# A 4-layer graph network on one core: the first transposes of 26 of 32 states go from TensorE to VectorE and DRAM, and the written-out order is chosen from sixteen

## The chip, the cores and the metric

The kernel runs on one core of a Trainium2 chip, in float32. The metric is the device time of one execution in microseconds (us), as a median of three runs. Five engines work side by side, each through its own list of instructions, in order: TensorE (PE in the profile, its weight loads PEld), VectorE (DVE), ScalarE (ACT), GpSimd (POOL) and SyncE (SP), which here issues nearly all DMAs. Within an engine nothing overtakes; between engines semaphores make an instruction wait for what it reads.

## The reference

32 states `x[b]` of 512 tokens x 128 features pass four residual layers that share one 512 x 512 adjacency. Each layer begins with a layer norm and a relu. Cut to what matters here:

```python
# layer 0
h = relu(layernorm(x));  x = x + (A_norm @ h) @ W.T + b
# layer 1: five recurrent steps, in_matrix and out_matrix are both adj
h = relu(layernorm(x))
for _ in range(5):
    m  = adj @ h;  av = concat([m, m])
    u3 = h @ u3_w.T + u3_b
    z  = sigmoid(av @ w3_w.T + w3_b + u3)
    r  = sigmoid(av @ w4_w.T + w4_b + u3)
    hv = tanh(av @ w5_w.T + w5_b + (r * h) @ u5_w.T + u5_b)
    h  = (1 - z) * h + z * hv
x = x + h
# layers 2 and 3: attention over the edges of adj (softmax), then x = x + elu(out) or x + out
```

## The kernel before

**Forms of a state.** A state is kept with tokens on partitions (`x`, `h`) or with features on partitions (`hT`). The products with the adjacency read `h` and give `m`, which has features on partitions; the gates of a recurrent step read `m` and `hT`. So each state needs both forms at the beginning of layer 1, and each of the first four steps has to turn its new `hT` back into an `h`.

**Layer 0 (`gcn`, L526).** States go in pairs. The first pair (states 0 and 1) uses `product` (L516): for each state four matmuls 128x512 against `anT`, then one ScalarE copy. All other pairs use `products` (L461): two states together in seven block products instead of eight, by sums and differences. That takes 14 matmuls 128x256 for the pair, four VectorE combinations (`combine`, L473), three VectorE sums (`add_up`, L498) and four ScalarE copies (`copy`, L490), and needs four factors made beforehand from `anT` or `adjT` (`right_factors`, L309). A float32 matmul appears as two records in the profile; a transpose is one.

**Layer 1 (`ggnn`, L547, and `step`, L565).** At the start, `norm_relu` (L400, ScalarE at L407) writes `h`. Then `to_features` (L426) turns it with four TensorE transposes 128x128 (L432) into a PSUM bank, and ScalarE copies the bank into `hT` (L555). Each of five steps does `products` for the pair with the `adjT` factors, and per state the gate matmuls L569, L570 (which reads `hT`), L576, L583, L584, three ScalarE tanhs (L572, L578, L586) and four VectorE operations (L574, L588, L589, L591). `shuttle` (L436) turns the new `hT` back without TensorE: VectorE transposes 32x32 squares into `sq` (L442), four DMAs write `sq` to the DRAM buffer `far` (L449), and two or one more DMAs read it into `h` (L453, L457). There are two `sq` buffers and four `far` buffers. At most six states are in layer 1 at a time (`LANES`), that is three pairs.

**Layers 2 and 3 (`gat`, L621)** use the same shuttle for the input (`gT`, L446, L457), and matmuls L644 and L699. The last four states (`NEAR`) use TensorE transposes there (L629, L664, L688), as does a last stretch of layer 1 if it is due late.

**What sets the order.** All instructions are first collected as operations with an engine, a cost, a delay until the result is seen, and a due time. `Plan.run` (L81) then plays the whole kernel through as a list scheduler: for each engine, the ready operation with the earliest due time goes next, if its buffers are free. A due time is lowered to `last - tail * hurry` where that is earlier; `tail` is the length of the chain that follows, and `last` and `hurry` are 174 and 0.08 (L201). The order that comes out is the order in which every engine's instructions are written; the costs are the planner's own, the chip only gets the order. Each DMA is planned with a delay of 4 us (into `far`) or 5 us (out of it). Recurrent VectorE work has a due time 5 ahead of its step, ScalarE's has the step's own.

Of the kernel before, what the change touches and what calls it, by code (L numbers as in the profile page):

```python
# [2 lines left out]

# [15 lines left out]
W = 32  # L19
Q = P // W  # L20
NEAR = 4
EASE = 0
LANES = 6


# [17 lines left out]
class Plan:  # L43
# [2 lines left out]

    DELAY = {"PE": 0.24, "ACT": 0.15, "DVE": 0.12, "POOL": 0.1, "SP": 2.4, "AQ": 2.4}

    def __init__(self, buffers, last, hurry):
        self.buffers, self.last, self.hurry, self.ops = buffers, last, hurry, []  # L50

    def op(self, engine, cost, due, emit, r=(), w=(), delay=None):
        o = Op(engine, cost, due, emit, self.DELAY[engine] if delay is None else delay)
# [25 lines left out]
        self.ops.append(o)  # L79

    def run(self):  # L81
        free = {k: list(reversed(v)) for k, v in self.buffers.items()}
        ready = {e: [] for e in self.DELAY}
        busy = dict.fromkeys(self.DELAY, False)
        events, order, done = [], [], 0

        for o in reversed(self.ops):
            o.tail = o.cost + o.delay + max((q.tail for q in o.then), default=0)
            o.due = min(o.due, self.last - o.tail * self.hurry)
        for o in self.ops:  # L90
            if not o.waits:
                heapq.heappush(ready[o.engine], (o.due, o.id))
        now, count = 0.0, 0

        def post(t, kind, x):
            nonlocal count
            count += 1
            heapq.heappush(events, (t, count, kind, x))

        def start(e):  # L100
            if busy[e]:
                return
            kept = []
            while ready[e]:
                key = heapq.heappop(ready[e])
                o = self.ops[key[1]]
                opens = [v for v in o.vals if v.kind and v.t is None]
                short = [v for v in opens if len(free[v.kind]) < sum(u.kind == v.kind for u in opens)]
                if not short:
                    for v in opens:  # L110
                        v.t = free[v.kind].pop()
                    busy[e] = True
                    o.at = now
                    order.append(o)
                    post(now + o.cost, 0, o)
                    post(now + o.cost + o.delay, 1, o)
                    break
                kept.append(key)
            for key in kept:
                heapq.heappush(ready[e], key)  # L120

        def settle(o, same):
            for q in o.then:
                if (q.engine == o.engine == "PE") == same:
                    q.waits -= 1
                    if not q.waits:
                        heapq.heappush(ready[q.engine], (q.due, q.id))

        for e in ready:
            start(e)  # L130
        while events:
            now, _, kind, o = heapq.heappop(events)
            if kind == 0:
                busy[o.engine] = False
                settle(o, True)
            else:
                done += 1
                settle(o, False)
                for v in o.vals:
                    v.uses -= 1  # L140
                    if not v.uses and v.kind:
                        free[v.kind].append(v.t)
            for e in ready:
                start(e)
        assert done == len(self.ops), "the order has come to a stop"
        self.order, self.end = order, now
        for o in order:
            o.emit()


@with_exitstack
def gnn_stack(ctx: ExitStack, tc: tile.TileContext, a: dict, out: bass.AP):
# [13 lines left out]
    def flat(t):  # L166
# [31 lines left out]
        "rstd": tiles(8, SMALL, "rstd"),  # L198
        "off": tiles(4, SMALL, "off"),
        "rden": tiles(3, SMALL, "rden"),  # L200
    }, 174, 0.08)  # L201
    op = plan.op
    MM, MM1, TURN = 0.858, 0.224, 0.111
    V, A = 0.61, 0.585
# [94 lines left out]
    def right_factors(mT, due):  # L299
# [10 lines left out]
                f[k][0](), quarter(*u), quarter(0, 1) if v is None else f[v][0]()),  # L310
               r=[mT, *([f[v][1]] if v else [])], w=[f[k][1]])
        return f
    of_adj, of_an = right_factors(adjT, -3), right_factors(anT, -1)


    maskT = {l: fixed([P, Q, N], f"maskT{l}", C, dtype=BF16) for l in (2, 3)}
# [119 lines left out]
    def shuttle(src, squares, dst, halves, due, soon):  # L436
# [19 lines left out]
        else:  # L456
            op("SP", 0.4, due, lambda: nc.sync.dma_start(  # L457
                dst.t if dst.kind != "h" else dst.t.rearrange("p a (k f) -> p (a k) f", k=2), far.t.rearrange("q i k f -> (q i) k f")),
               r=[far], w=[dst], delay=5)

    def products(h1, h2, factors, due):  # L461

        x1, x2, S = (h1[0], h1[1]), (h2[0], h2[1]), Val("S", 4)
        HV, HM, HA = 0.34, 2 * 0.432, 0.26

        def part(item):
            v, a = item
            return v.t[:, a, :]  # L470

        def combine(o, u, v, f):
            op("DVE", HV, due - 5, lambda: f(part(o), part(u), part(v)), r=[u, v], w=[o])  # L473
        add, sub = nc.vector.tensor_add, nc.vector.tensor_sub
        combine(S[2], x1[0], x2[0], sub)
        combine(S[0], x2[0], x2[1], add)
        combine(S[1], S[0], x1[0], sub)
        combine(S[3], x1[1], S[1], sub)
        m1, m2, p1, u2, u4, r, t = Val("m", 2), Val("m", 2), Val("half"), Val("half"), Val("half"), Val("bank"), Val("bank")

        def times(r, item, k, fresh, *also):
            def two():
                u = part(item).rearrange("p (f l) -> p l f", l=2)
                for l in range(2):
                    nc.tensor.matmul(low(r), u[:, l, :], factors[k][0]()[:, l, :], start=fresh and l == 0, stop=l == 1,  # L485
                                     skip_group_check=not fresh)
            op("PE", HM, due, two, r=[item, factors[k][1]], w=[r, *also])

        def copy(o, r, out):
            op("ACT", HA, due, lambda: nc.scalar.copy(out(), low(r)), r=[r], w=[o])  # L490

        def low(v):
            return flat(v.t)[:, :2 * P]

        def high(v):
            return flat(v.t)[:, 2 * P:]
        def add_up(o, u, out):
            op("DVE", HV, due - 5, lambda: nc.vector.tensor_add(out(), u.t, low(t)), r=[u, t], w=[o])  # L498

        times(r, x1[0], 0, True, m1, m2, t, p1, u2, u4)  # L500
        copy(p1, r, lambda: p1.t)
        times(t, x1[1], 3, True)
        add_up(m1[0], p1, lambda: low(m1))
        times(r, S[1], 1, False)
        copy(u2, r, lambda: u2.t)
        times(t, S[2], 4, True)
        times(r, S[0], 2, False)
        copy(u4, r, lambda: u4.t)
        add_up(m2[1], u4, lambda: high(m2))
        times(t, x2[1], 6, False)  # L510
        add_up(m2[0], u2, lambda: low(m2))
        times(r, S[3], 5, False)
        copy(m1[1], r, lambda: high(m1))
        return m1, m2
# [9 lines left out]


    def gcn(pair, due):  # L526
        first, ys = pair[0] == 0, []
        for i, b in enumerate(pair):
            y = Val("y", C) if first else Val("pair", 2)
            norm_relu(b, y, 2 * b - 798 if first else due + i)  # L530
            op("DVE", V, due + i + 1, lambda b=b: nc.vector.tensor_add(
                xs[b].t, xs[b].t, b0.t[:, None, :].to_broadcast([P, C, D])), r=[b0], w=[xs[b]])
            ys.append(y)

        ms = [product(y, anT, due + i + 1) for i, y in enumerate(ys)] if first else products(*ys, of_an, due + 1)
        for i, (b, m) in enumerate(zip(pair, ms)):
            p = Val("bank")

            def out_mm(m=m, p=p):
                for c in range(C):  # L540
                    nc.tensor.matmul(p.t[:, c, :], m.t[:, c, :], w0T.t[:, 0, :], start=True, stop=True)  # L541
            op("PE", C * MM1, due + i + 1.5, out_mm, r=[m, w0T], w=[p])
            op("DVE", V, due + i + 1.5, lambda b=b, p=p: nc.vector.tensor_add(flat(xs[b].t), flat(xs[b].t), flat(p.t)),
               r=[p], w=[xs[b]])


    def ggnn(pair, due):  # L547
        hs, hTs, lanes = [], [], []
        for b in pair:
            lane, h, hT = Val("lane"), Val("h", 2), Val("hT")  # L550
            op("SP", 0.0, due - 3, lambda: None, r=[xs[b]], w=[lane], delay=0)
            op("SP", 0.0, due - 3, lambda: None, r=[lane], w=[h], delay=0)
            norm_relu(b, h, due - 3)
            p = to_features(h, due - 2, hT)
            op("ACT", A, due - 2, lambda p=p, hT=hT: nc.scalar.copy(flat(hT.t), flat(p.t)), r=[p], w=[hT])  # L555
            hs.append(h)
            hTs.append(hT)
            lanes.append(lane)
# [6 lines left out]
    def step(b, s, m, hT, due, lane):  # L565
        gate, r, rh, z = Val("bank"), Val("r"), Val("rh"), Val("z")

        def reset():
            nc.tensor.matmul(flat(gate.t), gates.t[:, 0, :], flat(m.t), start=True, stop=False)  # L569
            nc.tensor.matmul(flat(gate.t), gates.t[:, 1, :], flat(hT.t), start=False, stop=True)  # L570
        op("PE", 2 * MM, due + 0.2, reset, r=[m, hT, gates], w=[gate])
        op("ACT", A, due, lambda: nc.scalar.activation(flat(r.t), flat(gate.t), AF.Tanh, bias=gate_b["w4"].t, scale=0.5),  # L572
           r=[gate, gate_b["w4"]], w=[r])
        op("DVE", V, due - 5, lambda: nc.vector.scalar_tensor_tensor(flat(rh.t), flat(r.t), 1.0, flat(hT.t), op0=ALU.add, op1=ALU.mult),  # L574
           r=[r, hT], w=[rh])
        op("PE", MM, due + 0.3, lambda: nc.tensor.matmul(flat(gate.t), gates.t[:, 2, :], flat(m.t), start=False, stop=True,  # L576
                                                   skip_group_check=True), r=[m, gates], w=[gate])
        op("ACT", A, due, lambda: nc.scalar.activation(flat(z.t), flat(gate.t), AF.Tanh, bias=gate_b["w3"].t, scale=0.5),  # L578
           r=[gate, gate_b["w3"]], w=[z])
        cand, hv, new = Val("bank"), Val("hv"), Val("hT")  # L580

        def candidate():
            nc.tensor.matmul(flat(cand.t), gates.t[:, 3, :], flat(m.t), start=True, stop=False)  # L583
            nc.tensor.matmul(flat(cand.t), u5T.t[:, 0, :], flat(rh.t), start=False, stop=True)  # L584
        op("PE", 2 * MM, due + 0.4, candidate, r=[m, rh, gates, u5T], w=[cand])
        op("ACT", A, due, lambda: nc.scalar.activation(flat(hv.t), flat(cand.t), AF.Tanh, bias=gate_b["w5"].t),  # L586
           r=[cand, z, gate_b["w5"]], w=[hv])
        op("DVE", V, due - 5, lambda: nc.vector.tensor_sub(flat(hv.t), flat(hv.t), flat(hT.t)), r=[hT], w=[hv])  # L588
        op("DVE", V, due - 5, lambda: nc.vector.scalar_tensor_tensor(flat(hv.t), flat(z.t), 1.0, flat(hv.t), op0=ALU.add, op1=ALU.mult),  # L589
# [172 lines left out]
```

## Time and profile before

| | us |
|---|---|
| median of 3 runs | 1664.14 (1663.68 to 1665.16) |
| profiled execution, its own time | 1663.59 |
| its span, first to last instruction | 1661.8 |
| PE busy | 1634.7 |
| DVE busy | 1362.7 |
| ACT busy | 734.8 |
| POOL busy | 143.2 |

A busy time counts every moment in which at least one instruction of the engine is running. Matmuls overlap in the PE, so a row's mean duration (such as 593 ns) is longer than the distance from one matmul to the next. That distance has to be read from the starts in the timeline. "Idle before" in a row is the time that the engine had nothing running before the row's instructions, and the arrow names what ended it.

### The profile page before, as it was taken

To read this page: it belongs to the slowest core of one execution; us is meant where nothing else is said; L and a number is where in the kernel's file an instruction comes from. 1 tells how busy PE (TensorE), PEld (TensorE's weight loads), DVE (VectorE), ACT (ScalarE), POOL (GpSimd) and SP (SyncE) were. 2 spreads that over 40 slices of the span, in tenths; PEclk is the share of its full clock that TensorE was granted. 3 is DMA by queue.
4 is the path that set the end of the run, shared out by engine and by line. 5 is a ranking of instruction groups with operands and counts; after the bars stand their busy time and mean duration, and the time that the engine had idled before them with its cause. 6 is when DMAs were issued, how large, how long until landed. Compare 5 with 4: busy or idle time off the path is not lost.

```text
span 1661.8 us, 23750 instructions
## 1 busy us (share of the span) xinstructions
PE 1634.7 (98%) x7422; PEld 1176.3 (71%) x7422; DVE 1362.7 (82%) x3836; ACT 734.8 (44%) x1657; POOL 143.2 (9%) x136
## 2 busy tenths in 40 slices
PE   7999999999999999999999999999999999999998
PEld 5766667677776777777677776777777777766677
DVE  8966778888878888888788888888888878777888
ACT  4643453535345354433534335353443534333433
POOL 2200000001001110000100000000000000000100
PEclk9999999999999999999999999999999999999999
DMA  5222333433334343342423334333242423434100
GB/s 153 51 70 58 83 83 95 115 80 99 90 89 108 84 105 87 91 113 73 122 71 99 98 92 108 90 96 95 77 121 64 108 70 91 106 90 114 27 26 27
DMA packets 311423, 146.17 MB, mean 88 GB/s; under 512 B 150400, under 2 KB 292864, under 8 KB 311296
## 3 DMA queue, kind: packets, MB, share of 16 engines
q1 hardware_dynamic: 311008, 144.12, 34.4%
q8 instruction: 59, 0.97, 0.2%
q14 instruction: 68, 0.56, 0.1%
q10 hardware_dynamic: 288, 0.52, 0.1%
HBM read 80.48 MB, written 64.08 MB: 87 GB/s over the span
## 4 chain that ended last, share of the span: by engine, by line
PE 92%; DVE 5%; ACT 1%; issue 1%; DMA 0%; POOL 0%; SPq 0%; DVEq 0%; POOLq 0%; ACTq 0%
PE bank L485 33%; PE bank L699 12%; PE bank L570 8%; PE bank L569 8%; PE bank L576 8%; PE bank L583 8%; PE bank L584 8%; PE bank L644 3%; PE bank L541 2%; PE bank L688 1%; PE bank L432 1%; DVE st L390 1%; PE bank L520 0%; ACT y L407 0%; POOL rstd L397 0%
## 5 line engine op out<-in xcount | busy, mean ns | idle before, releaser
L485 PE MATMUL bank<-made,S 128*128 128x256 f32 x1140 | 276.3, 380 | 3.9 <-DVE S L473 1.8
L397 POOL TENSOR_TENSOR rstd<-ve,mhalf 128x4 f32<-128x4 f32 x128 | 141.4, 1107 | 1491.0 <-DVE ve L395 1193.6
L485 PEld LDWEIGHTS bank<-made,S 128*128 128x128 f32 x1140 | 218.1, 196 | 45.5 <-issue 19.0
L490 ACT COPY half<-bank 128x256 f32<-128x256 f32 x285 | 105.3, 370 | 256.9 <-PE bank L485 254.9
L699 PEld LDWEIGHTS bank<-h_gat,e 128*128 128x128 f32 x1792 | 208.1, 192 | 12.7 <-issue 10.8
L572 ACT ACTIVATE r<-bank,gate_bw 128x512 f32<-128x512 f32 x160 | 109.6, 686 | 230.0 <-PE bank L570 218.7
L699 PE MATMUL bank<-h_gat,e 128*128 128x129 f32 x1792 | 208.5, 275 | 0.0
L574 DVE SCALAR_TENSOR_TENSOR rh<-r,hT 128x512 f32<-128x512 f32 x160 | 109.8, 687 | 100.6 <-ACT r L572 99.9
L679 DVE SCALAR_TENSOR_TENSOR e<-row,h_gat,maskT 128x512 f32<-128x512 f32 x256 | 181.3, 742 | 2.8 <-ACT row L666 2.8
L588 DVE TENSOR_TENSOR hv<-hv,hT 128x512 f32<-128x512 f32 x160 | 109.4, 683 | 67.6 <-ACT hv L586 67.2
L576 PE MATMUL bank<-m,wT 128*128 128x512 f32 x320 | 163.7, 593 | 0.0
L583 PE MATMUL bank<-m,wT 128*128 128x512 f32 x320 | 163.6, 593 | 0.0
L569 PE MATMUL bank<-m,wT 128*128 128x512 f32 x320 | 163.4, 592 | 0.0
L570 PE MATMUL bank<-hT,wT 128*128 128x512 f32 x320 | 163.4, 592 | 0.0
L584 PE MATMUL bank<-rh,wT 128*128 128x512 f32 x320 | 163.4, 592 | 0.0
L586 ACT ACTIVATE hv<-bank,gate_bw 128x512 f32<-128x512 f32 x160 | 109.5, 684 | 118.7 <-PE bank L584 117.5
L485 PE MATMUL bank<-adjT,h 128*128 128x256 f32 x640 | 157.8, 380 | 1.5 <-ACT h L407 1.5
L498 DVE TENSOR_TENSOR m<-half,bank 128x256 f32<-128x256 f32 x285 | 117.6, 413 | 43.2 <-ACT half L490 22.8
L485 PEld LDWEIGHTS bank<-adjT,h 128*128 128x128 f32 x640 | 121.7, 196 | 25.9 <-issue 12.1
L578 ACT ACTIVATE z<-bank,gate_bw 128x512 f32<-128x512 f32 x160 | 109.5, 684 | 49.5 <-PE bank L576 48.2
L390 DVE BATCH_NORM_STATS2 st<-x 128x6 f32<-128x128 f32 x512 | 121.6, 278 | 0.4
L570 PEld LDWEIGHTS bank<-hT,wT 128*128 128x128 f32 x320 | 60.8, 190 | 76.5 <-issue 76.5
(116 smaller groups left out, 2247.6 us busy)
## 6 DMA issues: line engine op xcount, KB each, us to landing
far<-sq SPq DMA_DIRECT2D x832, 64.0 KB
h<-far SPq DMA_DIRECT2D x248, 128.0 KB
gT<-far SPq DMA_DIRECT2D x56, 256.0 KB
row<-line SPq DMA_DIRECT2D x56, 256.0 KB
x<-in_x_dram SPq DMA_DIRECT2D x32, 256.0 KB
out_dram<-x SPq DMA_DIRECT2D x32, 256.0 KB
h<-far SPq DMA_DIRECT2D x28, 256.0 KB
far_mask<-mask SPq DMA_DIRECT2D x8, 128.0 KB
```

Of the source, the lines that this page charges most:

```text
L390: op("DVE", 0.21, due, lambda c=c: nc.vector.bn_stats(st.t[:, c, :], xb.t[:, c, :]), r=[xb[c]], w=[st[c]])
L397: op("POOL", 1.0, due, lambda: nc.gpsimd.tensor_tensor(rstd.t, ve.t, mhalf.t, ALU.pow), r=[ve, mhalf], w=[rstd])
L485: nc.tensor.matmul(low(r), u[:, l, :], factors[k][0]()[:, l, :], start=fresh and l == 0, stop=l == 1, skip_group_check=not fresh)
L498: op("DVE", HV, due - 5, lambda: nc.vector.tensor_add(out(), u.t, low(t)), r=[u, t], w=[o])
L569: nc.tensor.matmul(flat(gate.t), gates.t[:, 0, :], flat(m.t), start=True, stop=False)
L570: nc.tensor.matmul(flat(gate.t), gates.t[:, 1, :], flat(hT.t), start=False, stop=True)
L574: op("DVE", V, due - 5, lambda: nc.vector.scalar_tensor_tensor(flat(rh.t), flat(r.t), 1.0, flat(hT.t), op0=ALU.add, op1=ALU.mult), r=[r, h ...
L576: op("PE", MM, due + 0.3, lambda: nc.tensor.matmul(flat(gate.t), gates.t[:, 2, :], flat(m.t), start=False, stop=True, skip_group_check=Tru ...
L583: nc.tensor.matmul(flat(cand.t), gates.t[:, 3, :], flat(m.t), start=True, stop=False)
L584: nc.tensor.matmul(flat(cand.t), u5T.t[:, 0, :], flat(rh.t), start=False, stop=True)
L679: op("DVE", 0.68, due + 3, lambda j=j: nc.vector.scalar_tensor_tensor(e.t[:, j, :], row.t, h.t[:, j, D + 1:D + 2], maskT[l].t[:, j, :], op ...
L699: nc.tensor.matmul(pt()[:, c, :D + 1], e.t[:, j, i * P:(i + 1) * P], h.t[:, j, :D + 1], start=(j == 0), stop=(j == C - 1))
```

## The change

1. **First state by squares and DRAM.** For the states 2 to 27 (`FAR0 <= b < B - FAR1`) the transposes and the copy into `hT` are replaced by the new `shuttle_first`: two VectorE transposes of 32x32 squares from `h` to `sq`, four DMAs from `sq` to `far`, four DMAs from `far` to `hT`. States 0, 1 and 28 to 31 stay as they were. `hT` now has four parts, one for each DMA.
2. **Second pair in full.** States 2 and 3 use `product` with full matmuls in layer 0, like 0 and 1, and take their normed input from the two `y` buffers. The factors made from `anT` are due at 5 instead of -1.
3. **ScalarE ahead.** The recurrent tanhs are due 5 earlier, the copies in `products` 6 earlier.
4. **Order.** The planner tries sixteen pairs of `last` and `hurry` (170, 173, 176, 179 by 0.06, 0.08, 0.1, 0.12) and writes out the order that ends first by its own costs.

```diff
+FAR0, FAR1 = 2, 4
...
+        uses = {v: v.uses for o in self.ops for v in o.vals}
+        best = min(self.ends, key=lambda end: self.attempt(uses, *end))
+        self.attempt(uses, *best)
...
+    def attempt(self, uses, last, hurry):
...
+            o.soon = min(o.due, last - o.tail * hurry)
...
-    }, 174, 0.08)
+    }, [(last, hurry) for last in (170, 173, 176, 179) for hurry in (0.06, 0.08, 0.1, 0.12)])
...
-    of_adj, of_an = right_factors(adjT, -3), right_factors(anT, -1)
+    of_adj, of_an = right_factors(adjT, -3), right_factors(anT, 5)
...
+    def shuttle_first(h, hT, due, soon):
+
+        sq, far = Val("sq"), Val("far", Q)
+        for a in range(2):
+            op("DVE", 0.34, soon, lambda a=a: nc.vector.transpose(
+                sq.t.rearrange("p k (a l i) -> p a k l i", a=2, l=2)[:, a],
+                h.t.rearrange("p a (k j l) -> p a k l j", k=Q, l=2)[:, a]), r=[h[a]], w=[sq])
+        for q in range(Q):
+            op("SP", 0.44, due, lambda q=q: nc.sync.dma_start(
+                far.t[:, :, q, :].rearrange("k j f -> j k f"), sq.t[q * W:(q + 1) * W]), r=[sq], w=[far[q]], delay=4)
+        for q in range(Q):
+            op("SP", 0.4, due, lambda q=q: nc.sync.dma_start(
+                hT.t.rearrange("p c (q i) -> q p c i", q=Q)[q], far.t.rearrange("k j q (c i) -> q (k j) c i", c=C)[q]),
+               r=[far[q]], w=[hT[q]], delay=5)
...
-            op("ACT", HA, due, lambda: nc.scalar.copy(out(), low(r)), r=[r], w=[o])
+            op("ACT", HA, due - 6, lambda: nc.scalar.copy(out(), low(r)), r=[r], w=[o])
...
-        first, ys = pair[0] == 0, []
+        first, ys = pair[0] < 4, []
...
-            norm_relu(b, y, 2 * b - 798 if first else due + i)
+            norm_relu(b, y, 2 * b - 798 if pair[0] == 0 else due + i)
...
-            lane, h, hT = Val("lane"), Val("h", 2), Val("hT")
+            lane, h, hT = Val("lane"), Val("h", 2), Val("hT", Q)
...
-            p = to_features(h, due - 2, hT)
-            op("ACT", A, due - 2, lambda p=p, hT=hT: nc.scalar.copy(flat(hT.t), flat(p.t)), r=[p], w=[hT])
+            if FAR0 <= b < B - FAR1:
+                shuttle_first(h, hT, due - 2.5, due - 3)
+            else:
+                p = to_features(h, due - 2, hT)
+                op("ACT", A, due - 2, lambda p=p, hT=hT: nc.scalar.copy(flat(hT.t), flat(p.t)), r=[p], w=[hT])
...
-        op("ACT", A, due, lambda: nc.scalar.activation(flat(r.t), flat(gate.t), AF.Tanh, bias=gate_b["w4"].t, scale=0.5),
+        op("ACT", A, due - 5, lambda: nc.scalar.activation(flat(r.t), flat(gate.t), AF.Tanh, bias=gate_b["w4"].t, scale=0.5),
...
```

The tanhs of `z` and `hv` get the same `due - 5`.

More of the change, by code (lines that the diff above doesn't have):

```diff
@@ L1 @@
 import heapq
+import math
 from contextlib import ExitStack
@@ L47, with __init__ @@
     DELAY = {"PE": 0.24, "ACT": 0.15, "DVE": 0.12, "POOL": 0.1, "SP": 2.4, "AQ": 2.4}
-    def __init__(self, buffers, last, hurry):
-        self.buffers, self.last, self.hurry, self.ops = buffers, last, hurry, []
+    def __init__(self, buffers, ends):
+        self.buffers, self.ends, self.ops = buffers, ends, []
     def op(self, engine, cost, due, emit, r=(), w=(), delay=None):
@@ L81, in run @@
     def run(self):
+        for o in reversed(self.ops):
+            o.tail = o.cost + o.delay + max((q.tail for q in o.then), default=0)
+            o.first = o.waits
+        uses = {v: v.uses for o in self.ops for v in o.vals}
+        best = min(self.ends, key=lambda end: self.attempt(uses, *end))
+        self.attempt(uses, *best)
+        assert self.end < math.inf, "the order has come to a stop"
+        for o in self.order:
+            o.emit()
+    def attempt(self, uses, last, hurry):
+        for v, n in uses.items():
+            v.uses = n
+            if v.kind:
+                v.t = None
+        for o in self.ops:
+            o.waits = o.first
+            o.soon = min(o.due, last - o.tail * hurry)
         free = {k: list(reversed(v)) for k, v in self.buffers.items()}
@@ L85, in run @@
         events, order, done = [], [], 0
-        for o in reversed(self.ops):
-            o.tail = o.cost + o.delay + max((q.tail for q in o.then), default=0)
-            o.due = min(o.due, self.last - o.tail * self.hurry)
         for o in self.ops:
             if not o.waits:
-                heapq.heappush(ready[o.engine], (o.due, o.id))
+                heapq.heappush(ready[o.engine], (o.soon, o.id))
         now, count = 0.0, 0
@@ L126, in settle @@
                     if not q.waits:
-                        heapq.heappush(ready[q.engine], (q.due, q.id))
+                        heapq.heappush(ready[q.engine], (q.soon, q.id))
         for e in ready:
@@ L144, in run @@
                 start(e)
[L145 to L148, printed above, removed]
+        self.order, self.end = order, now if done == len(self.ops) else math.inf
+        return self.end
 @with_exitstack
@@ L577, in step @@
                                                    skip_group_check=True), r=[m, gates], w=[gate])
-        op("ACT", A, due, lambda: nc.scalar.activation(flat(z.t), flat(gate.t), AF.Tanh, bias=gate_b["w3"].t, scale=0.5),
+        op("ACT", A, due - 5, lambda: nc.scalar.activation(flat(z.t), flat(gate.t), AF.Tanh, bias=gate_b["w3"].t, scale=0.5),
            r=[gate, gate_b["w3"]], w=[z])
@@ L585, in step @@
         op("PE", 2 * MM, due + 0.4, candidate, r=[m, rh, gates, u5T], w=[cand])
-        op("ACT", A, due, lambda: nc.scalar.activation(flat(hv.t), flat(cand.t), AF.Tanh, bias=gate_b["w5"].t),
+        op("ACT", A, due - 5, lambda: nc.scalar.activation(flat(hv.t), flat(cand.t), AF.Tanh, bias=gate_b["w5"].t),
            r=[cand, z, gate_b["w5"]], w=[hv])
```

## The prediction

> **What bounds the kernel now.** I read the page's busy times first, then the busy times by stage.
>
> ```profile
> PE 1634.7 (98%) x7422; PEld 1176.3 (71%) x7422; DVE 1362.7 (82%) x3836; ACT 734.8 (44%) x1657; POOL 143.2 (9%) x136
> ...
> PE 92%; DVE 5%; ACT 1%; issue 1%; DMA 0%; POOL 0%; SPq 0%; DVEq 0%; POOLq 0%; ACTq 0%
> ```
>
> ```profile
> 0.00:20.00 20.00, 13.36 (x65) 9.96 (x66) 13.36 (x48) 8.95 (x20) 3.79 (x10) 1.00 0.74 209
> 20.00:40.00 20.00, 16.51 (x69) 11.64 (x68) 19.49 (x89) 10.08 (x25) 5.21 (x5) 1.00 0.30 90
> 40.00:60.00 20.00, 20.00 (x88) 14.98 (x87) 19.74 (x77) 14.35 (x34) 5.00 (x6) 1.00 0.40 103
> 60.00:80.00 20.00, 20.00 (x91) 16.11 (x90) 19.33 (x95) 13.18 (x33) 8.20 (x8) 1.00 0.09 21
> 300.00:1300.00 1000.00, 999.40 (x4562) 722.76 (x4561) 843.14 (x2370) 442.52 (x1001) 86.07 (x79) 1.00 0.38 95
> ```
>
> The columns are PE, PEld, DVE, ACT, POOL, clock, DMA share. From 300 to 1300 us the PE is idle for 0.6 us in 1000. It loses time at the ends: 10.1 us before 37 us, some 3.9 us between 1500 and 1570, and 10.8 us after 1612 (of which 4.9 lie behind the last matmul). Busy does not mean full speed, so I looked at the starts in the timeline of PE:
>
> ```profile
> 503.72 1.03 PE L485 MATMUL bank<-made,S 128*128 128x256 f32 x4
> 504.58 1.11 PE L432 MATMUL bank<-ident,h 128*128 128x128 f32 x8
> 505.53 1.90 PE L485 MATMUL bank<-adjT,h 128*128 128x256 f32 x8
> 507.27 1.04 PE L485 MATMUL bank<-adjT,S 128*128 128x256 f32 x4
> ```
>
> [...] The starts speak otherwise: four records start 0.86 us before the next row, eight 1.74 us, that is 0.215 to 0.2175 apart, without a hole. PE is full, by order and not only by record. I take the starts: a microsecond of work taken from PE between 40 and 1500 us is a microsecond off the end, as long as the others deliver.
>
> **The change part by part.**
>
> *First state, PE.* The eight transposes above are two states and occupy 505.53 - 504.58 = 0.95 us of PE. 26 of 32 states lose theirs: 13 x 0.95 = 12.35 us off PE. Four transposes alone take 0.43 us elsewhere (1544.57 to 1545.00), which would give 11.2; I take the row in the steady part. ScalarE loses 26 copies (L555, 586 ns), 15.2 us, worth nothing by itself: ScalarE is 44% busy and its waits are mostly for PE.
>
> *First state, DVE.* 52 square transposes are added. The nearest row is the same operation on a state of the same size:
>
> ```profile
> L432 PE MATMUL bank<-ident,h 128*128 128x128 f32 x128 | 19.8, 283 | 0.6 <-ACT h L407 0.6
> L555 ACT COPY hT<-bank 128x512 f32<-128x512 f32 x32 | 18.1, 586 | 1.9 <-PE bank L432 1.3
> L442 DVE STREAM_TRANSPOSE sq<-hT 128x256 f32<-128x256 f32 x248 | 105.5, 433 | 1.4
> ```
>
> 52 x 0.433 = 22.5 us. DVE in the middle is 84.3% busy; with 19 states there (76 of the 104 transposes) it gets 16.5 us more in about 990, 86.7%. Between 40 and 80 us DVE was 98% busy and PE still 100%, so this is covered. Without that cover, each state would hold PE for its two transposes, 0.87 us, 22.5 us in all. A gain is excluded for an added operation. Ends 0 and 22.5; the 40 to 80 us rows are the nearest, I take +0.5.
>
> *First state, SP and DMA.* 208 DMAs are added: 104 into `far` (L449, median 434 ns of SP) and 104 out of it with 512 pieces each (as L453, 524 ns): 45 + 54 = 99 us of issue. SP's two great groups now take 832 x 0.434 + 248 x 0.524 = 491 us of 1662, so the queue has room. It is in order, though: behind an L449 that waits stand the next `h` of other lanes (L453), the rows (L676), outputs (L721) and loads of `x` (L239). Such waits exist already:
>
> ```profile
> SPq L449 <- DVE sq L442: 189.6, 70, 16.4
> ...
> SPq L449 <- DMA h<-far: 83.9, 42, 2.8
> ```
>
> (total, times, longest). Waits up to 16.4 us there reach PE nowhere in the middle, where PE waits 0.6 us in all and not for a DMA. Two `sq` and four `far` buffers serve 124 + 84 = 208 shuttles; they get 26 more, an eighth. I put SP at 0.
>
> ```profile
> DMA packets 311423, 146.17 MB, mean 88 GB/s; under 512 B 150400, under 2 KB 292864, under 8 KB 311296
> ...
> q1 hardware_dynamic: 311008, 144.12, 34.4%
> ```
>
> 34.4% of 16 engines x 1661.8 us over 311,008 packets is 29.4 ns each. The last step writes `hT` in runs of 32 floats, 128 B: 2048 packets for a state, with 512 more into `far`. 26 x 2560 x 29.4 ns / 16 = 122 us, so the share rises by 7 points to 42%. One DMA of 512 packets needs 0.94 us. [...] The rows show 208 such turns in 1662 us, with runs of 256 B and more, at 34%. The squares are turned on DVE; the DMA moves whole runs. I take the trace.
>
> *The new wait.* L570 of a pair's first step will wait for DMAs instead of ScalarE. From `h`: 0.87 us on DVE; from the first L449 to the issue of L453 3.2 us (50.39 to 53.62); four issues 2.1; landing 2.8 by the longest wait above: 9.0 us. PE has the pair's seven products in between, 28 records x 0.2175 = 6.1 us; the other 2.9 us must come from the two other pairs in the lanes. The planner allows 4 and 5 us for the DMAs, more than these rows show, so its order leaves that room. Uncovered it would cost 13 x 2.9 = 38 us; I take 0. Queued behind a waiting L570 is all of PE.
>
> *Second pair.* Seven products, 28 x 0.2175 = 6.09 us, become eight matmuls 128x512, 16 records: four last from 18.90 to 20.61, 0.4275 each, 6.84. PE +0.75. DVE loses four combinations and three sums (7 x 0.41 = 2.9), and the four `anT` factors (683 ns each) move behind the first states, 2.7 us out of a stretch where DVE was 97% busy (20 to 40 us) and PE idle for 3.5. PE's waits from 24 us to 37 are 1.45, 0.22, 0.38, 0.19 and 0.50 us, 2.7 in all: the most to be gained. Two more states in the two `y` buffers and two shuttles may cost as much. I take -1.0.
>
> *ScalarE ahead, and the order.* No instruction is added. 860 ScalarE instructions get earlier due times than 480 norm-relus (L407) and the attention's L646, L673, L714; no DMA and no POOL work moves with them. PE's waits for ScalarE sum to some 8 us over the whole span, so this gains at most that; cover is ScalarE's 56% idle time, and without it norms come late. The choice among sixteen can reach PE's 5.9 us of waiting after 1612 and 3.9 at 1500 to 1570, about -9, and may miss by as much, since it goes by planned costs (V = 0.61 where the rows have 0.68). I take -0.5 for both together, near zero because no row shows it.
>
> *Sum.* -12.35 + 0.75 + 0.5 - 1.0 - 0.5 = -12.6 us. The profiled execution took 1663.59 us (span 1661.8 and 1.8 around it), so 1651.0; the median is 0.55 above that execution, so about 1651.5.
>
> **The rivals.**
>
> *DVE becomes the bound in places* (0.09). For: 98% at 20 to 80 us, its real operations longer than planned. Against: PE fed without a gap there. Half of the far end, 11 us, would come back: 1651.5 - 0.5 + 11 = 1662, or a third (7.5 us): about 1658.5. I put it at 1658 to 1662.
>
> *The order gives much more* (0.11). ScalarE ahead shortens the last states' recurrence, and the startup runs denser; of 5.9 + 3.9 + 2.7 us some 8 go instead of 1.5: 1645.
>
> *Slower: the first `hT` comes late* (0.03). One mechanism, at L570 of thirteen pairs: 2.9 us uncovered gives 1651.5 + 38 = 1689; slower from 12.6 / 13 = 0.97 us for a pair on. For: two `far` waits of 2.8 us exist, and small packets. Against: the planner's allowance.
>
> *The change does not do what it says* (0.02): the order chosen for its planned end is worse by 12 us on the chip than the one before: 1664. It would have to lose more than all waits at the end.
>
> **How the numbers follow.** The forecast has 0.75, with its own range 1647 to 1656. The range that should hold 8 in 10 takes in most of the better order and part of the DVE case: 1645 to 1659.5. A difference of 0.2%, 3.3 us, is about what a measurement of this kernel can tell from no change. Faster: 0.75 + 0.11 + two thirds of 0.09 = 0.92. Same: a third of 0.09 and the last rival, with some of the slower one's small end: 0.05. Slower: 0.03.
>
> **What would show it.** Right: L432 with h at 24 records instead of 128, L555 at 6, PE busy near 1621, PE again 99.9% in the middle, DVE near 86%, DMA share near 42%. Wrong: a wait of PE or PEld at L570 for a DMA `hT<-far` above a few us in total, SP waiting for `far` for hundreds of us with PE idle, or PE idle in the middle by over 5 us with DVE named. A time under 1645 would mean that the ends, not the transposes, brought most.

## The result, and the profile after

The changed kernel takes 1647.05 us (median of 5 runs, 1646.67 to 1649.17), the kernel before 1664.12 us beside it. The ratio is 0.9901, with a 95% interval of 0.9887 to 0.9915. The forecast was 1651.5 (1645.0 to 1659.5): right in direction and inside the range, but the gain is 17.1 us where 12.6 were added up. The profiled execution has a span of 1645.1 us, 16.7 less than before.

The page of the changed kernel: busy times, the chain that ended last, and the DMA queue that carries the shuttles.

```profile
PE 1620.7 (99%) x7306; PEld 1159.8 (71%) x7306; DVE 1373.5 (83%) x3881; ACT 722.0 (44%) x1629; POOL 144.6 (9%) x136
...
DMA packets 381312, 159.81 MB, mean 97 GB/s; under 512 B 206976, under 2 KB 362752, under 8 KB 381184
...
q1 hardware_dynamic: 380896, 157.77, 39.4%
...
PE 94%; DVE 4%; DMA 1%; issue 0%; ACT 0%; SPq 0%; DVEq 0%
```

PE's busy time fell by 14.0 us, to the 1621 of the forecast. DVE's rose by 10.8. The DMA share rose by 5.0 points, not 7: 69,888 packets more (2688 a state, where the forecast had 2560), but 0.394 x 16 x 1645.1 / 380,896 = 27.2 ns each instead of 29.4.

The groups of instructions of the changed kernel that stand for the first states (line, operation, count, busy, mean, idle before):

```profile
L448 PE MATMUL bank<-ident,h 128*128 128x128 f32 x24 | 3.5, 281 | 0.0
L589 ACT COPY hT<-bank 128x512 f32<-128x512 f32 x6 | 3.4, 580 | 0.2
L481 DVE STREAM_TRANSPOSE sq<-h 128x256 f32<-128x256 f32 x52 | 21.9, 432 | 0.1
```

24 transposes of `h` are left of 128, 6 copies of 32, and the 52 new squares last 432 ns each, as their neighbours did. The stages of the changed kernel (PE, PEld, DVE, ACT, POOL, clock, DMA share, GB/s; the clock is the granted share of TensorE's full clock):

```profile
0.00:20.00 20.00, 13.58 (x64) 10.57 (x65) 12.46 (x47) 8.75 (x20) 3.79 (x10) 1.00 0.76 211
20.00:40.00 20.00, 18.97 (x78) 12.50 (x77) 19.52 (x87) 10.17 (x26) 4.61 (x5) 1.00 0.30 85
40.00:60.00 20.00, 18.89 (x68) 11.79 (x67) 18.79 (x77) 12.59 (x30) 5.61 (x6) 1.00 0.56 135
60.00:80.00 20.00, 19.79 (x85) 14.85 (x84) 19.72 (x85) 11.95 (x31) 4.95 (x6) 1.00 0.43 87
300.00:1300.00 1000.00, 1000.00 (x4509) 719.53 (x4508) 863.36 (x2450) 447.95 (x1017) 92.19 (x82) 1.00 0.44 107
```

PE is busy for 18.97 us of the second 20 instead of 16.51. It gives 1.3 us of that back from 40 to 80, where it was full before. Between 300 and 1300 its records leave no gap. DVE is at 86.3% there, as forecast. SP's waits (total, times, longest):

```profile
SPq L465 <- DVE sq L458: 191.1, 63, 14.2
...
SPq L465 <- DMA h<-far: 67.6, 29, 3.7
...
SPq L485 <- DVE sq L481: 14.0, 7, 3.7
```

The old shuttles wait about as long as before for squares (191 us, 190 before) and less for a free `far` (68, 84 before). The new ones (L485) wait 14 us for squares and have no such row for `far`.

**A sharper measure than busy time.** A 128x256 record lasts 380 ns, but the next one starts 216 ns later. A hole of up to 0.16 us between two starts hides under the record. So I counted the work: the number of records of each shape times the distance of their starts in unbroken rows (0.2159 us for 128x256, 0.4295 for 128x512, 0.1116 for 128x129, 0.1118 for 128x131, 0.1105 for 128x128; the kernel before has 2660, 1616, 2048, 512 and 582 of them, the changed one 2632, 1632, 2048, 512 and 478). What a stretch lasts beyond that is loss, visible or not, and matmuls that run at a lower clock count as loss too. "Start" is the first 100 us, "end" the last 160 us, "middle" all between. A record cut by a border counts on both sides, so the sums are good to 1 us.

| kernel, profiled execution | span | work | loss at the start | in the middle | at the end |
|---|---|---|---|---|---|
| before | 1661.8 | 1618.8 | 15.3 | 7.2 | 20.2 |
| changed | 1645.1 | 1608.2 | 14.5 | 3.4 | 18.1 |
| difference | -16.7 | -10.6 | -0.8 | -3.8 | -2.1 |

The forecast had -11.6 for work, -1.0 for the start, +0.5 in the middle, -0.5 for the order. The middle brought most of the surprise, the end some. The experiments ask what did it.

### The profile page after: what moved, and what is told of

It is laid out like the page before. It is cut to its first block, busy times and chain, and to the rows that moved or that the text cites. A ratio compares the mean times of both kernels' runs of the same rounds, so it can differ in the third digit from the quotient of the medians.

```text
span 1645.1 us, 23871 instructions
## 1 busy us (share of the span) xinstructions
PE 1620.7 (99%) x7306; PEld 1159.8 (71%) x7306; DVE 1373.5 (83%) x3881; ACT 722.0 (44%) x1629; POOL 144.6 (9%) x136
## 3 DMA queue, kind: packets, MB, share of 16 engines
q1 hardware_dynamic: 380896, 157.77, 39.4%
## 4 chain that ended last, share of the span: by engine, by line
PE 94%; DVE 4%; DMA 1%; issue 0%; ACT 0%; SPq 0%; DVEq 0%
PE bank L516 34%; PE bank L733 12%; PE bank L603 8%; PE bank L604 8%; PE bank L617 8%; PE bank L610 8%; PE bank L618 8%; PE bank L678 3%; PE bank L572 1%; PE bank L722 1%; DVE e L713 1%; DVE st L406 1%; PE bank L705 0%; PE bank L448 0%; DVE y L432 0%
## 5 line engine op out<-in xcount | busy, mean ns | idle before, releaser
L516 PE MATMUL bank<-made,S 128*128 128x256 f32 x1128 | 270.3, 380 | 1.6 <-DVE S L504 0.7
L733 PEld LDWEIGHTS bank<-h_gat,e 128*128 128x128 f32 x1792 | 208.2, 192 | 17.4 <-issue 14.8
L604 PE MATMUL bank<-hT,wT 128*128 128x512 f32 x320 | 163.4, 592 | 0.0
L516 PE MATMUL bank<-adjT,h 128*128 128x256 f32 x640 | 161.6, 380 | 0.6 <-ACT h L423 0.3
L423 ACT ACTIVATE y<-x,off,rstd 128x128 f32<-128x128 f32 x240 | 104.5, 485 | 26.9 <-DVE off L420 25.0
```

The source lines that it names most:

```text
L733: nc.tensor.matmul(pt()[:, c, :D + 1], e.t[:, j, i * P:(i + 1) * P], h.t[:, j, :D + 1], start=(j == 0), stop=(j == C - 1))
```

## The experiments

Each kernel below is a variant of the changed one. "Middle" and "end" are losses counted as above.

**1. The price of the transposes, at an unchanged order.** The planner's choice is replaced by the pair it had chosen, and the transposes come back as work that nobody reads.

```diff
-    }, [(last, hurry) for last in (170, 173, 176, 179) for hurry in (0.06, 0.08, 0.1, 0.12)])
+    }, [(176, 0.1)])
...
         def reset():
+            for c in range(C if s == 0 and FAR0 <= b < B - FAR1 else 0):
+                nc.tensor.transpose(gate.t[:, c, :], block(adjT.t, c), ident.t)
```

> The changed kernel in exactly its order (last 176, hurry 0.1 given), but with four TensorE transposes put back ahead of the first gate matmul of each of the 26 states, into the bank that this matmul then overwrites; they transpose blocks of adjT and are read by nobody. 104 transposes are the only difference. If TensorE is the bound, the time rises by their slots, 104 x 0.1105 to 0.119 = 11.5 to 12.4 us, to 1658.5 to 1659.5. If they were partly hidden (TensorE not the bound), by less than 9.

Measured: 1658.69 us (1658.18 to 1659.3), 11.6 more than the changed kernel, 0.112 us for each of 104 transposes. Middle 3.6, end 19.2: all of it is work. TensorE is the bound, and a microsecond put on it is a microsecond at the end. The forecast's price of 12.35 was 0.7 too high, because its row held eight transposes, 0.884 us by the distances above, and lasted 0.95.

**2. The choice of order, taken away.**

```diff
-    }, [(last, hurry) for last in (170, 173, 176, 179) for hurry in (0.06, 0.08, 0.1, 0.12)])
+    }, [(174, 0.08)])
```

> All of the change except the choice of order: the plan is made once, with last 174 and hurry 0.08 as in the kernel before. Theory O (order): the forecast left out that the choice of order is worth some 5 to 7 us, so this takes 1652 to 1654 us. Theory W (work): the change wins by TensorE work and a denser middle alone, and the choice is worth at most 1.5 us, so this takes 1647 to 1648.5.

Measured: 1655.58 us (1654.87 to 1656.37), 8.5 more than the changed kernel, and a little more than theory O expected. Work and middle are the same (1608.2 and 3.4), the start is 1.5 better (13.0), the end is 9.4 worse (27.5). The stretches from 160 us before the end, of the changed kernel and then of this one:

```profile
1485.00:1645.10 160.10, 146.15 (x875) 114.64 (x873) 130.15 (x372) 61.22 (x156) 13.30 (x12) 0.99 0.19 47
```

```profile
1493.00:1653.40 160.40, 141.18 (x825) 112.09 (x823) 122.49 (x342) 56.81 (x146) 10.87 (x10) 0.95 0.16 42
```

The same 160 us hold 875 matmul records with the chosen order and 825 without. The remaining states run out of independent work, and PE waits for DVE, longest for the attention's `e` (5.3 us). The waits are not all. In two pieces of that stretch, each behind such a hole (2.97 and 5.34 us), the granted clock is 0.50:

```profile
1595.40:1605.60 10.20, 7.46 (x30) 6.35 (x31) 9.55 (x41) 2.17 (x6) 3.41 (x3) 0.50 0.01 2
1622.70:1629.50 6.80, 3.67 (x17) 3.67 (x18) 6.70 (x36) 0.60 (x1) 3.45 (x3) 0.50 0.01 2
```

By the distances above the matmuls in them are worth 5.2 us. At half the clock they cost that once more, over half of the 9.4: an estimate from eight transposes there, which took 1.92 us and take 1.04 elsewhere. In the changed kernel's profile no matmul runs at less than the full clock (1.00 from 1500 to 1640 us; the last matmul ends at 1640.1). The last section takes this up.

**3. The choice alone, on the kernel before.**

```diff
-FAR0, FAR1 = 2, 4
+FAR0, FAR1 = 32, 4
...
-    of_adj, of_an = right_factors(adjT, -3), right_factors(anT, 5)
+    of_adj, of_an = right_factors(adjT, -3), right_factors(anT, -1)
...
-        first, ys = pair[0] < 4, []
+        first, ys = pair[0] == 0, []
...
-            op("ACT", HA, due - 6, lambda: nc.scalar.copy(out(), low(r)), r=[r], w=[o])
+            op("ACT", HA, due, lambda: nc.scalar.copy(out(), low(r)), r=[r], w=[o])
```

(`due - 5` of the three tanhs becomes `due` too.)

> The kernel before with the choice of sixteen alone: no first states by squares, no full second pair, no earlier ScalarE due times. If the choice has a fixed worth of its own (theory O in its simple form, 5 to 7 us), 1657 to 1659 us. If it is worth something only together with the other parts, because the order before was already a good one for its own work, 1663 to 1665.

Measured: 1664.68 us, ratio to the kernel before 1.0001 (0.9993 to 1.0009). The choice is worth nothing where the single order was good already: end 20.6 against 20.2. It is worth 8.5 us where the other edits had spoilt the end.

**4. The order that the planner puts last.**

```diff
-    }, [(last, hurry) for last in (170, 173, 176, 179) for hurry in (0.06, 0.08, 0.1, 0.12)])
+    }, [(170, 0.1)])
```

> The changed kernel in the order of last 170, hurry 0.1, which the planner's own costs put last of the sixteen. Theory O: the planned ends hold on the chip, this is 8 to 14 us slower than the changed kernel: 1655 to 1661 us, with the loss in holes of TensorE. Theory W: orders differ little on the chip, 1646 to 1650.

Measured: 1661.21 us (1660.18 to 1662.12), 14.2 more than the changed kernel; middle 3.7, end 32.6. On the chip the planner's last of sixteen is far behind its first, the fixed (174, 0.08) lies between. The planner ranks these three orders rightly (played through from the kernel file, without the chip, it ends them at 1640.0, 1647.0 and 1652.4), and they differ nearly at the end alone. Here too two pieces at a clock of 0.50 hold matmuls worth 5.8 us (mean clock 0.66 from 1580 to 1600 us and again from 1615 to 1630).

**5. The squares twice, at an unchanged order.**

```diff
-    }, [(last, hurry) for last in (170, 173, 176, 179) for hurry in (0.06, 0.08, 0.1, 0.12)])
+    }, [(176, 0.1)])
...
-            op("DVE", 0.34, soon, lambda a=a: nc.vector.transpose(
+            op("DVE", 0.34, soon, lambda a=a: [nc.vector.transpose(
...
-                h.t.rearrange("p a (k j l) -> p a k l j", k=Q, l=2)[:, a]), r=[h[a]], w=[sq])
+                h.t.rearrange("p a (k j l) -> p a k l j", k=Q, l=2)[:, a]) for _ in range(2)], r=[h[a]], w=[sq])
```

> The changed kernel in its own order, with each of the 52 new square transposes on VectorE done twice (the second writes the same values): 22.5 us more of VectorE work in the places where the change put it. If VectorE's load is covered, as the forecast took it (0.5 us), at most 1 us: 1647 to 1648. If VectorE holds TensorE back for each state (the forecast's far end), up to 22 us, 1655 and more.

Measured: 1661.27 us (1658.88 to 1662.15), 14.2 more: 0.63 us for each us of VectorE work that the order had not planned for. Of these, 10.2 are in the middle, which loses 13.6 instead of 3.4; at the end the clock takes part (last section). The page's PE idle does not show it all. Its stages from 100 us to 160 us before the end:

```profile
100.00:300.00 200.00, 198.58 (x754) 132.17 (x753) 146.42 (x354) 85.75 (x175) 8.06 (x7) 1.00 0.34 81
300.00:1500.00 1200.00, 1194.88 (x5349) 852.91 (x5348) 1030.91 (x2872) 524.52 (x1183) 101.39 (x90) 1.00 0.43 104
```

The records leave 1.4 + 5.1 = 6.5 us idle; counted by starts, 13.6 are lost, all of them at the full clock. And DVE is at 85.9%: with 14% idle it holds PE up. The forecast's argument from the stretch of 40 to 80 us, where DVE was 98% busy and PE full, does not carry over. There the plan had other work for PE at hand.

**6. Squares and ScalarE, two by two.** If the doubled squares cost so much, why did the single ones not? The next kernels leave out ScalarE's earlier due times, then the squares, and then, with the second pair gone as well, one of the two or neither. First the changed kernel without ScalarE ahead:

```diff
-            op("ACT", HA, due - 6, lambda: nc.scalar.copy(out(), low(r)), r=[r], w=[o])
+            op("ACT", HA, due, lambda: nc.scalar.copy(out(), low(r)), r=[r], w=[o])
...
-        op("ACT", A, due - 5, lambda: nc.scalar.activation(flat(r.t), flat(gate.t), AF.Tanh, bias=gate_b["w4"].t, scale=0.5),
+        op("ACT", A, due, lambda: nc.scalar.activation(flat(r.t), flat(gate.t), AF.Tanh, bias=gate_b["w4"].t, scale=0.5),
```

> The changed kernel without the earlier ScalarE due times, best of sixteen. In the changed kernel TensorE loses 3.4 us between 100 us and 160 us before the end, before it lost 7.2. Theory S: the earlier due times took those 3.8 us, so here the middle loses about 7 again, and the time is 1651 to 1656, with what the end makes of it. Theory F: the first states by squares took them (no ScalarE copy and no PSUM bank for a first state), so the middle stays near 3.5 and only the end decides: 1646 to 1656.

Measured: 1658.0 us (1657.18 to 1658.48), 11.0 more; middle 13.5, nearly twice what theory S said and above the 7.2 of the kernel before. The timeline of ACT in this kernel, and PE's in the same moment:

```profile
799.92 1.65 ACT L423 ACTIVATE y<-x,off,rstd 128x128 f32<-128x128 f32 x4 [0.56 <-DVE off L420]
801.47 0.87 ACT L423 ACTIVATE h<-x,off,rstd 128x128 f32<-128x128 f32 x2
802.24 1.63 ACT L423 ACTIVATE y<-x,off,rstd 128x128 f32<-128x128 f32 x4
803.78 0.48 ACT L423 ACTIVATE h<-x,off,rstd 128x128 f32<-128x128 f32 x1
804.16 0.35 ACT L521 COPY half<-bank 128x256 f32<-128x256 f32 x1
```

```profile
799.57 1.03 PE L516 MATMUL bank<-adjT,h 128*128 128x256 f32 x4
804.57 1.65 PE L516 MATMUL bank<-adjT,S 128*128 128x256 f32 x3 [3.97 <-ACT half L521]
```

PE's last row before the hole starts at 799.57. The copy that the next one waits for stands on ACT behind eleven norm-relus, which last some 4.2 us, and the first of which has itself waited for `off` from DVE. PE waits 3.97 us. With ScalarE's due times of the step itself, the norms (due at 87) are written ahead of the recurrent copy (due at 88); when they come late, the copy is late, and TensorE stands. What follows the hole is also lost time. The clock is halved there (0.50), and the matmuls in this stretch are worth 3.0 us by their distances:

```profile
803.30:810.10 6.80, 5.54 (x13) 4.47 (x14) 3.85 (x16) 3.14 (x10) 0.86 (x1) 0.50 0.72 173
```

So this one place takes 7.0 of the middle's 13.5 us (3.97, and 3.0 estimated as in experiment 2). The other 6.5 are about what the kernel before loses. Nor is it a delay on the chip: the planner's own play of this kernel has a PE hole of 4.28 us at the same copy, behind the same norms. That the squares are what brings it about is an inference from the kernels below, not from this row.

Now the changed kernel without the squares:

```diff
-FAR0, FAR1 = 2, 4
+FAR0, FAR1 = 32, 4
```

> The changed kernel with TensorE transposes for all first states, best of sixteen (the second pair and ScalarE ahead stay). By TensorE's work alone 11.6 us more than the changed kernel: 1658.5 (as with the transposes put back in the same order, 1658.7). Theory F says 3 to 4 more, 1662, with a middle that loses about 7 us; theory S says the middle stays near 3.5. The end of the newly chosen order may add or take 4 us.

Measured: 1659.81 us (1659.51 to 1661.05), 12.8 more, of which 11.5 are work. Middle 3.3: theory F falls, the squares did not empty the middle, ScalarE did. The start is 2.0 better, the end 3.4 worse.

The same pair of edits on the kernel before, each alone with the choice of sixteen:

> The kernel before with the first states by squares and the choice of sixteen; no full second pair, no earlier ScalarE due times. Theory I (interaction): the squares load VectorE so that, without ScalarE ahead, TensorE's middle loses 13 to 14 us instead of 7.6; so of the 11.6 us of transposes only about 5 arrive: 1658 to 1660. Theory W: each part has its own worth, 1653 to 1654.

> The kernel before with ScalarE's earlier due times and the choice of sixteen; no first states by squares, no full second pair. Theory I: the middle loses about 3.5 us instead of 7.6, so 1660 to 1661. If ScalarE ahead by itself is worth its whole 10 us (as the kernel without it suggests), 1654 to 1656. If it is worth nothing without the squares, 1664 to 1665.

And both together, which is the changed kernel without the second pair:

```diff
-    of_adj, of_an = right_factors(adjT, -3), right_factors(anT, 5)
+    of_adj, of_an = right_factors(adjT, -3), right_factors(anT, -1)
...
-        first, ys = pair[0] < 4, []
+        first, ys = pair[0] == 0, []
```

> The changed kernel with the second pair in seven products again and the anT factors due at -1, best of sixteen. TensorE has 0.8 us less work; by the forecast the startup then loses 1 to 2.7 us more (VectorE makes the factors first, TensorE waits as before between 24 and 37 us): 1647.5 to 1649. If the second pair is worth nothing, 1646 to 1647.

| all with the choice of sixteen | time | work | middle | start | end |
|---|---|---|---|---|---|
| neither (experiment 3) | 1664.68 | 1618.8 | 7.6 | 15.1 | 20.6 |
| squares | 1659.87 | 1607.3 | 12.9 | 16.2 | 21.5 |
| ScalarE ahead | 1662.22 | 1618.8 | 3.5 | 16.4 | 21.3 |
| both | 1649.85 | 1607.3 | 2.9 | 15.6 | 20.9 |

By themselves the squares bring 4.8 us and ScalarE 2.5, together 14.8. The planner's own ends (1656.8, 1649.5, 1653.1 and 1641.5, in the table's order) hold the same interaction: 7.3 and 3.7 alone, 15.3 together. The squares take 11.5 us of work off TensorE, but alone they give 5.3 back in the middle (7.6 to 12.9). The kernel with the squares alone names its waits in the middle (total, times, longest), and its clock behind the longest one:

```profile
PE bank L516 <- ACT half L521: 6.8, 7, 4.0
PE bank L572 <- ACT m L521: 0.5, 1, 0.5
```

```profile
808.30:811.70 3.40, 3.40 (x10) 2.69 (x9) 1.78 (x7) 0.97 (x3) 0.00 (x0) 0.50 0.65 151
```

It is the same copy and the same hole again: 3.97 us, and matmuls worth 1.7 at half the clock, 5.7 together. Without them the middle would lose 7.2, no more than with neither part. The plans agree: both kernels with squares and without ScalarE ahead have the hole of 4.28 us in theirs, and none of the other plans in this document has a PE hole over 1 us in the middle. So what the squares give back is one place in the order, with the clock behind it, and not a load that is felt everywhere. With ScalarE ahead that place is gone (2.9, against 3.5 without squares). Theory I holds for the middle, and theory W, that each part has a worth of its own, falls. Two of these times lie a little above their expected bands: ScalarE alone by 1.2 us, through start and end, and both together by 0.85.

The second pair: from 1649.85 to 1647.05 it brings 2.8 us. It costs 0.9 of work, the start gains 1.1, so about nothing in its own place, as forecast (-0.25). The rest is an end shorter by 2.8, and this is not shown to be the second pair's. The planner leaves PE as long idle in the last 160 us of both plans (11.8 us), but without the second pair matmuls worth 4.3 us fall into pieces at half the clock (mean clock of the last 160 us 0.96), and in the changed kernel's profile none do (1.00 up to its last matmul). An execution of the changed kernel with a lower mean clock (0.997 instead of 0.999) took 1649.17 us, nearly as long as the four without the pair (0.996 to 0.997).

**7. Copies or tanhs?**

```diff
-        op("ACT", A, due - 5, lambda: nc.scalar.activation(flat(r.t), flat(gate.t), AF.Tanh, bias=gate_b["w4"].t, scale=0.5),
+        op("ACT", A, due, lambda: nc.scalar.activation(flat(r.t), flat(gate.t), AF.Tanh, bias=gate_b["w4"].t, scale=0.5),
```

(So for all three tanhs; the copies keep `due - 6`.)

> The changed kernel with only the copies in products due 6 earlier; the recurrent tanhs have their step's own due time again; best of sixteen. If the late copies alone starved TensorE (its waits in the middle without ScalarE ahead name this copy), the middle stays at 3 to 4.5 us and the time is 1647 to 1650. If the tanhs matter as much, the middle loses 7 to 10 us, 1651 to 1655.

Measured: 1649.31 us (1648.4 to 1650.05), middle 4.9. Of the 10.1 us that ScalarE ahead takes from the middle (13.5 to 3.4), the copies take 8.6; 7.0 of the 10.1 are the one hole and its clock.

**8. One step further.** If the transposes and the end are what is left, keep to squares a little longer in the last stretch.

```diff
-EASE = 0
+EASE = -5
...
-    }, [(last, hurry) for last in (170, 173, 176, 179) for hurry in (0.06, 0.08, 0.1, 0.12)])
+    }, [(176, 0.1)])
```

> The changed kernel in the order of last 176, hurry 0.1, with EASE -5: the recurrent steps keep to squares and DRAM until a due time of 165 instead of 160, so fewer TensorE transposes fall into the last stretch. If this stretch is still bound by TensorE's work and by the holes that the order leaves, 2 to 3 us better than the changed kernel, 1644 to 1645. If the shuttle's longer way (some 9 us by the forecast) delays the last states, as much worse, 1650.

Measured: 1645.24 us (1644.1 to 1646.28), ratio to the kernel before 0.9885 (0.987 to 0.99). Twelve transposes less (20 of `hT` instead of 32), work 1.4 less. The median is 1.8 us below the changed kernel's, but the intervals of the two ratios overlap, so this is probably better and not shown to be.

## Why the prediction was right or wrong

**TensorE as the bound: right.** Work fell by 10.6 us where 11.6 were forecast, and experiment 1 gives a full microsecond for each one: 11.6 us for 104 transposes, which the distances put at 11.5. The weight loads were busy for 71% before and after (1176.3 and 1159.8 us), and the transposes arrived in full all the same.

**"Without that cover ... Ends 0 and 22.5 ... I take +0.5" (the squares on DVE): mis-sized as a part of its own.** The squares alone cost the middle 5.3 us, all in one place of the order, and a second helping, which no order had planned for, 10.2. The step that failed is the cover: it was read from a busy share (98% and PE still full), and cover depends on what the order has at hand behind a late operation. In the change the cost was about 0, since ScalarE ahead took it away; that the total came out right in this term is luck, for a reason that the text did not have.

**"I take -0.5 for both together, near zero because no row shows it" (ScalarE ahead and the order): the term that failed.** ScalarE ahead takes 10.1 us from the middle in company with the squares and 4.1 without. The bound of 8 us came from PE's waits for ScalarE in the profile of before. It left out that the same change would make a new wait of this kind, and the slower matmuls behind it. The order is worth 8.5 us against the old `last` and `hurry`, and nothing on the kernel before. The forecast's silent assumption was that the old pair would end the new work as well as it had ended the old. It would have lost 7.3 us more at the end (27.5 against 20.2).

**What no row showed, the plan did.** The forecast took the planner's allowances for DMAs, but not its ends. Played through from the two kernel files, before any run, these are 1656.9 and 1640.0: 16.9 us less, where the chip gave 17.1. The sum of parts gave 12.6. Every kernel here whose work is all in its plan took 7.1 to 10.3 us more than its planned end, so the plan is good to about 3 us here, and it holds the interaction that a sum of parts cannot.

**The start: right in size.** -0.8 for the whole and -1.1 for the second pair by itself (experiment 6), -1.0 forecast; between 24 and 37 us PE now fills its old holes with the second pair's full products.

**The new wait at L570 (now L604), SP and DMA: right.** Everything that this line's weight load and matmul waited for, apart from issue, is one row of the changed kernel (time, times):

```profile
  DMA far<-sq: 0.5, 2
```

The slower rival, a late first `hT`, did not come. 208 more DMAs and small pieces (56,576 more packets under 512 B) changed the DMA share by 5 points (34.4% to 39.4%) and cost PE at most half a microsecond of waiting here.

**The rivals.** "DVE becomes the bound in places" was a live danger: without ScalarE ahead it is, by the inference of experiment 6, what the squares do in one place, and doubled squares do it all over the middle. "The order gives much more" named the right direction (1645), with the end as its place; most of what was missed lay in the middle.

## What to carry to other kernels

When work moves from the full engine to a half-idle one, look at what stands in order behind it: with VectorE fuller, norms stood on ScalarE ahead of a copy, and TensorE waited for the copy. One such place was worth an estimated 5.7 us in one kernel and 7.0 in another, the slower clock behind it included. Put the recurrent work of the engine between ahead of the work that can wait; the two edits here are worth 14.8 us together and 7.3 apart. And re-choose a tuned order after each change of the work: the old constants were as good as the best for the old kernel and 8.5 us worse for the new one. Where a planner writes the order, compare its own ends first; they cost no run.

## What the hardware showed that I had not expected

Some holes in TensorE were paid twice. In the kernel with one order (experiment 2), PE stood idle for 5.34 us near the end, and the matmuls after it ran slower:

```profile
1625.83 2.09 PE L722 MATMUL bank<-h_gat,e 128*128 128x129 f32 x8 [5.34 <-DVE e L713]
1627.71 1.92 PE L448 MATMUL bank<-ident,y 128*128 128x128 f32 x8
```

The second row of the two at 0.50 in experiment 2 is this stretch. Eight such transposes take 1.04 us elsewhere (the changed kernel's L698, 1630.53), eight such L722 1.05. Here they took 1.92 and 2.09, nearly twice as long. The profiles show 0.50 with other long holes too: in experiment 4 with 3.47 and 4.49 us before 1581.90 and 1589.22 (mean clock 0.66 from 1580 to 1600) and with 7.26 us before 1624.16 (0.66 from 1615 to 1630), and in experiment 6 with the two of 3.97 us.

Behind shorter holes they show both. Experiment 2 has 2.97 us before 1595.41, and its first row at 0.50 is behind that. The changed kernel has 3.07 us before 1623.48 and no such stretch: sixteen L722 took 2.05 us as ever. In experiment 5, whose order is the same, PE's longest wait for `e` at L722 is 3.1 us as well, but the mean clock of the last 160 us is 0.97, where the changed kernel has 0.99. There is one behind a row of short holes too: the kernel before has four of 0.41 to 1.24 us between 1634 and 1640, and a clock of 0.51 from 1640.2 to 1643.6.

So the clock differs between executions of one order too, and the time with it: of experiment 5's fourteen executions the two with a mean clock of 0.999 took 1658.88 and 1659.1 us, the nine with 0.997 took 1661.2 to 1662.15. Differences of 2 or 3 us between these kernels can be this alone, the second pair's 2.8 and experiment 8's 1.8 among them. And orders with holes can lose more than the holes, in experiment 2 an estimated 5.2 us more.
